# One state-space layer, re-planned: B and C sent out in a later step, the residual read late, seven decays ahead, moments in SBUF, one pair moved from GpSimd to VectorE

## The chip, the cores and the metric

The kernel runs on one core of a Trainium2 chip. A core has five engines that each take their instructions in order: TensorE (PE in the profile, with PEld for its weight loads), VectorE (DVE), ScalarE (ACT), GpSimd (POOL) and SyncE (SP), which here issues nearly all DMAs. They meet through semaphores: an instruction that waits holds up everything behind it on its engine. The metric is the device time of one execution in microseconds; less is better.

## What is computed

The input is x, of 4 images with 192 channels of 128 x 128 pixels. Layer 0 normalises x by groups and runs 1x1 convolutions, fractional Fourier transforms and inverse transforms on it. The second layer is a selective state-space block; the change touches only this one. The text calls it layer 2; in the code it is `layer1`. Cut to what matters:

```python
seq = layernorm(groupnorm(x))                    # tokens x 192
xs, z = split(seq @ in_proj_w.T)                 # 384 channels each
u  = silu(causal_conv4(xs) + conv_b)
dt, B, C = split(u @ x_proj_w.T)                 # rank 12, 16 states, 16 states
dt = softplus(dt @ dt_proj_w.T + dt_proj_b)
h[t] = h[t-1] * exp(dt[t] * A) + dt[t] * u[t] * B[t]     # 384 channels x 16 states
y[t] = sum over states of h[t] * C[t]  +  u[t] * D
out  = x + (y * silu(z)) @ out_proj_w.T
```

The recurrence in h runs over the 16,384 tokens of each image.

## The kernel before

Layer 2 goes through 128 chunks of 512 tokens (32 an image). The 384 channels are 3 blocks j of 128 partitions, the 16 states are 8 pairs sg. A chunk therefore has 24 steps k = 8 j + sg, and one step does a pair of states: two scans of 128 x 512 on VectorE (`scans`, L953), then one product of both with C on GpSimd (L966, `hc`), then sums over the states on TensorE three steps later (`sums`, L979, accumulated in PSUM by transposing). I number the states of a chunk 2 k and 2 k + 1.

A scan needs a decay exp(dt A) and an input dt u B. The decay is one Exp on ScalarE (L875). Where the input comes from is told by a letter in `KINDS`, one string of eight for each j:

- V: VectorE multiplies, one product of 128 x 512 for each state (`product`, L896), from a copy of dt u in PSUM (`dtu_copy`), two scans ahead.
- P: ScalarE scales a transposed dt u by B (`scale`, L924, tiles `dbT`, four for each state), and TensorE turns it back into PSUM (`turned_back`, L939), just ahead of its scan.
- O: GpSimd multiplies both states at once (`inputs`, L907, tile `db`), two steps ahead. Here the decay is written into PSUM (`decay_there`, tile `op`), three states ahead of its scan. For V and P it goes to SBUF (`early`, tile `da`), `AHEAD` = 4 decays ahead, into a ring of four.

The results of the scans, `h`, are in a ring of three, so step k waits until GpSimd and the carry's DMA have read h of step k - 3. The carry (L964) takes the last column of both scans out to the next chunk; it is a DMA of 1 KB on SP. B and C, of 64 KB, go out to DRAM (`xd_out`, L801) and come back spread over all partitions, 512 KB for each pair (`load_bc`, L844 and L848), behind the scans of steps 19 to 23 and 0 to 2.

Everything else is laid between these steps by a plan written out by hand. An entry of `PLAN` is a step, a phase, a function and its arguments. A step relative to a chunk's first one can be negative or over 23: the work of three chunks is interleaved. Inside a step the order is S (first), A (after the sums of an earlier step), then the first scan, M (between the two scans), the second scan, L (last). The work that the plan places for a chunk is, in its order: the load of x (`load_x`), the turn to tokens on TensorE, mean and variance (`moments`, L702 and L704), the reciprocal root by Ln and Exp (`rstd`), the normalising (`normed`, L725), the turn back to channels (`to_channels`), `channels` (L751; its second part also sends a shifted copy of `s` over SP, L757), the convolution (`conv`, L766), `silu_u` (L778), the gate's projection and activation (`proj_z` L772 and L773, `silu_z` L785), `proj_x` and `xd_out`, `proj_dt`, `softplus`, dt u on GpSimd (`dt_u`), the turns of B and of dt u, and at the end `evacuate` (`yt`, L988), `turn`, `gate` (L1011), `project_out` (L1018) and the residual's add (`add_x`, L1025) with the output's DMA (L1029).

ScalarE has Silu, Softplus and Exp with Ln in three different tables, so a change between them costs a table load. Five PSUM banks are handed from use to use in the order of the program, three more form the ring `op` for inputs and for the decays of kind O.

Of the kernel before, what the change touches and what calls it, by code (L numbers as in the profile page):

```python
# [10 lines left out]
F32 = mybir.dt.float32  # L11
I32 = mybir.dt.int32
BF16 = mybir.dt.bfloat16
AF = mybir.ActivationFunctionType
# [4 lines left out]
S = 128  # L19
C = 192  # L20
# [101 lines left out]
def layer0(tc, x, xmid, st2, w):  # L122
# [409 lines left out]

KINDS = ("VOPPVVOP", "VOVPOVPP", "VOVPPVOP")

PLAN = (
    (-35, "M", "load_x"), (-34, "M", "to_tokens", 1), (-34, "L", "to_tokens", 0),
    (-33, "L", "moments", 0), (-32, "A", "moments", 1), (-31, "L", "rstd"), (-30, "M", "shift"),
    (-30, "M", "normed", 0), (-30, "M", "normed", 1), (-30, "M", "to_channels", 1),  # L540
    (-29, "L", "to_channels", 0), (-29, "L", "channels", 0), (-27, "L", "channels", 1),
    (-26, "S", "conv", 0, 0), (-26, "L", "conv", 1, 0), (-25, "L", "conv", 1, 1),
    (-24, "L", "conv", 1, 2), (-22, "S", "conv", 0, 1), (-20, "S", "silu_u", 1),
    (-20, "S", "conv", 0, 2), (-20, "S", "silu_u", 0), (-20, "M", "conv", 2, 0),
    (-19, "M", "conv", 2, 1), (-17, "A", "conv", 2, 2), (-16, "L", "silu_u", 2),
    (-15, "L", "proj_z", 0), (-15, "L", "silu_z", 0), (-13, "S", "proj_x"), (-13, "M", "xd_out"),
    (-11, "M", "proj_dt"), (-10, "S", "softplus"), (-9, "M", "dt_u", 1), (-8, "S", "turn_b"),
    (-8, "M", "dt_u", 0), (-8, "M", "b_out"), (-4, "A", "turned", 0), (-2, "M", "scale", 0, 6),
    (-2, "L", "dtu_copy", 0), (-1, "A", "scale", 0, 4), (0, "A", "scale", 0, 5),
    (0, "M", "scale", 0, 15), (1, "S", "scale", 0, 7), (2, "M", "scale", 0, 14),  # L550
    (4, "S", "turned", 1), (7, "A", "dt_u", 2), (7, "A", "dtu_copy", 1), (7, "A", "scale", 1, 6),
    (7, "M", "scale", 1, 7), (9, "M", "scale", 1, 15), (10, "S", "proj_z", 1),
    (10, "A", "scale", 1, 14), (10, "L", "scale", 1, 13), (10, "L", "scale", 1, 12),
    (10, "L", "evacuate", 0), (11, "S", "proj_z", 2), (11, "M", "silu_z", 1),
    (11, "M", "silu_z", 2), (11, "L", "turn", 0), (13, "S", "gate", 0), (13, "A", "dtu_copy", 2),
    (17, "S", "turned", 2), (17, "S", "scale", 2, 6), (17, "M", "scale", 2, 7),
    (18, "M", "scale", 2, 8), (18, "M", "scale", 2, 9), (18, "M", "evacuate", 1),
    (19, "L", "scale", 2, 15), (20, "S", "scale", 2, 14), (21, "A", "turn", 1),
    (22, "S", "gate", 1), (27, "A", "evacuate", 2), (29, "S", "turn", 2), (29, "M", "gate", 2),
    (32, "S", "project_out", 0), (32, "L", "add_x", 0), (34, "S", "project_out", 1),  # L560
    (34, "L", "add_x", 1),
)

# [1 line left out]
def layer1(tc, xmid, out, st2, w, n_tok=S * S):  # L565
# [3 lines left out]
    NCHUNK = n_tok // T  # L569
    G = 2  # L570
    LAG, BCL = 3, 5
    AHEAD = 4
    NBLK = T // 128

    with ExitStack() as ctx:
# [26 lines left out]
        def done(g, *key):  # L602
            banks.append(g.pop(key)[1])
# [19 lines left out]
        for b in range(B):  # L623
            nc.sync.dma_start(
                out=gd[CH : CH + 1, b, :, :], in_=dnmr[:, b, :].rearrange("c t -> t c").unsqueeze(0)
            )
        xms = [cp.tile([CH + 1, 2, T], F32, name=f"xm{i}") for i in range(3)]
        for xm in xms:
            nc.vector.memset(xm[CH : CH + 1], 1.0)

        ln = const("ln")
        wz = cp.tile([128, 2, NJ, 128], F32, name="wz")
# [33 lines left out]
        def log_exp():  # L666
            if table[0] != "log_exp":
                nc.scalar.preload_act_table_set("natural_log_exp_and_others")  # L668
                table[0] = "log_exp"

        def load_x(i):
            b, ch = divmod(i, NCHUNK)
            xm = got[i]["xm"] = xms[i % 3]
            nc.sync.dma_start(
                out=xm[0:CH],
                in_=xmid[b][:, ch * T : (ch + 1) * T].rearrange("(t p) f -> p t f", p=CH),
            )

        def to_tokens(i, half):
            g = got[i]
            psum(g, "X", half)
            for blk in (2 * half, 2 * half + 1):
                for t in range(2):
                    nc.tensor.matmul(
                        row(g, blk)[:, t * CH : (t + 1) * CH],
                        g["xm"][:, t, blk * 128 : (blk + 1) * 128], gd[:, i // NCHUNK, t, :],
                        start=True, stop=True,
                    )  # L690

        def row(g, blk):
            return g["X", blk // 2][0][:, blk % 2 * C : (blk % 2 + 1) * C]

        def mean_var(g):
            return g["X", 1][0][:, 2 * C : 2 * C + 2 * NBLK].rearrange("p (k m) -> p k m", m=2)

        def moments(i, half):
            g = got[i]
            st = tp.tile([128, 2, 6], F32, name="st")  # L700
            for blk in range(2):
                nc.vector.bn_stats(st[:, blk, :], row(g, 2 * half + blk))  # L702
            for blk in range(2):
                nc.vector.bn_aggr(mean_var(g)[:, 2 * half + blk, :], st[:, blk, :])  # L704

        def rstd(i):
            g = got[i]
            rs = g["rs"] = tp.tile([128, NBLK], F32, name="rs")
            log_exp()
            nc.scalar.activation(rs, mean_var(g)[:, :, 1], AF.Ln, bias=eps)  # L710
            nc.scalar.activation(rs, rs, AF.Exp, scale=-0.5)

        def shift(i):
            g = got[i]
            sh = g["sh"] = tp.tile([128, NBLK], F32, name="sh")
            nc.vector.scalar_tensor_tensor(
                sh, mean_var(g)[:, :, 0], -1.0, g["rs"], ALU.mult, ALU.mult
            )

        def normed(i, half):  # L720
# [74 lines left out]
        def xd_out(i):  # L795
            g = got[i]
            xd = g["xd"] = tp.tile([128, T], F32, name="xd", bufs=1)
            nc.scalar.copy(xd, g["px",][0])
            done(g, "px")
            dbc = g["dbc"] = dram.tile([2, NS, T], F32, name="dbc")  # L800
            nc.sync.dma_start(out=dbc.rearrange("a s t -> (a s) t"), in_=xd[96:, :])  # L801

        def proj_dt(i):
            g = got[i]
# [3 lines left out]
                rows = slice(32 * j, 32 * j + RANK)  # L808
                nc.tensor.matmul(g["d", j][0], dtT[rows, :], g["xd"][rows, :], start=True, stop=True)

        def softplus(i):
            g = got[i]
            for j in range(NJ):
                g["dt", j] = jp.tile([128, T], F32, name="dt")
                nc.scalar.activation(g["dt", j], g["d", j][0], AF.Softplus, bias=dtb[:, j : j + 1])  # L815
                done(g, "d", j)
            table[0] = "softplus"

        def dt_u(i, j):
            g = got[i]  # L820
# [57 lines left out]
        def early(i):  # L878

            if i < len(own):  # L880
                decay(own[i], scp.tile([128, T], F32, name="da"))

        def decay_there(s):

# [56 lines left out]
        def scans(pos, n, k, between):  # L941
            g = got[n]
            j, sg = divmod(k, NG)
            ch = n % NCHUNK
            if k == 0:
                g["carry"] = tp.tile([128, NJ, NS], F32, name="carry")
                g["before"], last["carry"] = last.get("carry"), g["carry"]
            db = g.pop(("db", k), None)
            h = scp.tile([128, G, T], F32, name="h", bufs=3)
            for q in range(G):  # L950
                st = sg * G + q
                s = G * pos + q
                nc.vector.tensor_tensor_scan(  # L953
                    h[:, q, :], das.pop(s), dbs.pop(s) if db is None else db[:, q, :],
                    0.0 if ch == 0 else g["before"][:, j, st : st + 1], ALU.mult, ALU.add,
                )
                product(s + 2)
                decay_there(s + 3)
                if q == 0:
                    turned_back(s + 3)  # L960
                    between()
                if s in turns:
                    early(turns[s] + AHEAD)
            nc.sync.dma_start(out=g["carry"][:, j, sg * G : (sg + 1) * G], in_=h[:, :, T - 1])  # L964
            hc = scp.tile([128, G, T], F32, name="hc", bufs=5)
            nc.gpsimd.tensor_tensor(hc, h, g["c", "b", sg], ALU.mult)  # L966
            g["hc", k] = hc
# [53 lines left out]
                )  # L1021

        def add_x(n, t):
            xm = got[n]["xm"][0:CH]
            nc.vector.tensor_add(xm[:, t, :], got[n]["po", t][0][0:CH], xm[:, t, :])  # L1025
            done(got[n], "po", t)
            if t == 1:
                b, ch = divmod(n, NCHUNK)
                nc.sync.dma_start(  # L1029
                    out=out[b][:, ch * T : (ch + 1) * T].rearrange("(t p) f -> p t f", p=CH), in_=xm  # L1030
                )
                got[n] = None

        order = [(n, k) for n in range(total) for k in range(NGR)]
        does = dict(
            load_x=load_x, to_tokens=to_tokens, moments=moments, rstd=rstd, shift=shift,
            normed=normed, to_channels=to_channels, channels=channels, conv=conv, proj_z=proj_z,
            silu_u=silu_u, silu_z=silu_z, proj_x=proj_x, xd_out=xd_out, proj_dt=proj_dt, softplus=softplus, dt_u=dt_u,
            turn_b=turn_b, b_out=b_out, dtu_copy=dtu_copy, turned=turned, scale=scale,
            evacuate=evacuate, turn=turn, gate=gate, project_out=project_out, add_x=add_x,  # L1040
        )
# [193 lines left out]
```

## Time and profile before

| | |
|---|---|
| median of 3 runs | 11,175.64 us (11,174.62 to 11,181.45) |
| the profiled execution | 11,188.61 us, its span 11,186.7 us |
| first scan of layer 2 | 1,446 us after the span's start |
| scans L953, with a carry | 4,464 and 1,488, mean 1,268 and 1,267 ns |
| products with C, L966 | 3,072, mean 2,367 ns |
| products of kind O, L907 | 768, mean 2,373 ns |
| products of kind V, L896 | 2,304, mean 676 ns |
| scalings of kind P, L924 | 9,216, mean 396 ns |
| B, C loads to landing | 4.9 and 5.8 us |

A mean duration isn't the time that an instruction adds to a full engine: the next one begins before the last one ends. In the timeline, two scans follow each other at 1.18 us, a product behind a scan adds 0.59, a decay adds 0.615, and one dbT tile 0.25. Sums of work are made from such spacings. In the lines of waits the columns are the total in us, the number of waits and the longest one. In a timeline, the columns are the start, the length, the engine, the line, the operation and, in square brackets, the idle time before and who ended it.

### The profile page before, as it was taken

To read this page: it belongs to the slowest core of one execution; us is meant where nothing else is said; L and a number is where in the kernel's file an instruction comes from. 1 tells how busy PE (TensorE), PEld (TensorE's weight loads), DVE (VectorE), ACT (ScalarE), POOL (GpSimd) and SP (SyncE) were. 2 spreads that over 40 slices of the span, in tenths; PEclk is the share of its full clock that TensorE was granted. 3 is DMA by queue.
4 is the path that set the end of the run, shared out by engine and by line. 5 is a ranking of instruction groups with operands and counts; after the bars stand their busy time and mean duration, and the time that the engine had idled before them with its cause. 6 is when DMAs were issued, how large, how long until landed. Compare 5 with 4: busy or idle time off the path is not lost. (4 is left out here: it accounts for less than half of the span.)

```text
span 11186.7 us, 171424 instructions
## 1 busy us (share of the span) xinstructions
PE 9950.4 (89%) x56050; PEld 6911.8 (62%) x56050; DVE 10160.0 (91%) x11330; ACT 9542.3 (85%) x20197; POOL 9513.5 (85%) x4342
## 2 busy tenths in 40 slices
PE   4777789999999999999999999999999999999998
PEld 2434356666666666666666666666666666666666
DVE  5666679999999999999999999999999999999999
ACT  2333189999999999999999999999999999999998
POOL 0000079999999999999999999999999999999999
PEclk8888699999999999999999999999999999999999
DMA  8786733333333333333333333333343333333333
GB/s 234 187 225 163 220 98 114 117 105 109 117 105 110 117 105 109 117 112 102 118 117 97 119 119 95 118 119 99 114 119 101 113 117 106 109 117 107 107 117 92
DMA packets 1330364, 1366.48 MB, mean 122 GB/s; under 512 B 918346, under 2 KB 969791, under 8 KB 1328831
## 3 DMA queue, kind: packets, MB, share of 16 engines
q1 hardware_dynamic: 1308990, 1292.60, 39.8%
q0 software_dynamic: 13312, 50.34, 1.4%
q10 hardware_dynamic: 7168, 12.59, 0.3%
q8 instruction: 445, 7.29, 0.3%
q14 instruction: 449, 3.67, 0.1%
HBM read 1179.79 MB, written 155.33 MB: 119 GB/s over the span
## 5 line engine op out<-in xcount | busy, mean ns | idle before, releaser
L966 POOL TENSOR_TENSOR hc<-h,c 128x1024 f32<-128x1024 f32 x3072 | 7200.0, 2367 | 321.2 <-DVE h L953 240.8
L953 DVE TENSOR_TENSOR_SCAN h<-da,carry,op 128x512 f32<-128x512 f32 x4464 | 5532.7, 1268 | 281.0 <-ACT op L875 122.6
L875 ACT ACTIVATE da<-dt,c_A_log 128x512 f32<-128x512 f32 x4608 | 3218.5, 741 | 224.7 <-DVE h L953 216.0
L979 PE MATMUL ps<-ident,hc 128*128 128x128 f32 x24576 | 3258.2, 278 | 3.7 <-POOL hc L966 3.7
L979 PEld LDWEIGHTS ps<-ident,hc 128*128 128x128 f32 x24576 | 2874.5, 144 | 277.2 <-issue 272.2
L924 ACT ACTIVATE dbT<-ps,bT 128x128 f32<-128x128 f32 x9216 | 2583.6, 396 | 12.6 <-PE op L939 11.7
L766 PE MATMUL ps<-s,wc 128*128 128x512 f32 x4608 | 2184.4, 596 | 44.0 <-ACT u L778 36.4
L953 DVE TENSOR_TENSOR_SCAN h<-op,carry,db 128x512 f32<-128x512 f32 x1488 | 1853.4, 1267 | 98.0 <-DMA carry<-h 81.7
L907 POOL TENSOR_TENSOR db<-dtu,b 128x1024 f32<-128x1024 f32 x768 | 1822.5, 2373 | 7.4 <-DMA b<-dbc 7.4
L939 PE MATMUL op<-ident,dbT 128*128 128x128 f32 x9216 | 1422.6, 281 | 242.8 <-ACT dbT L924 168.8
L939 PEld LDWEIGHTS op<-ident,dbT 128*128 128x128 f32 x9216 | 1107.4, 144 | 752.1 <-issue 334.6
L896 DVE TENSOR_TENSOR op<-ps,b 128x512 f32<-128x512 f32 x2304 | 1556.5, 676 | 7.2 <-ACT ps L856 7.2
L875 ACT ACTIVATE op<-dt,c_A_log 128x512 f32<-128x512 f32 x1536 | 1092.0, 711 | 267.4 <-DVE h L953 267.2
L766 PEld LDWEIGHTS ps<-s,wc 128*128 128x128 f32 x4608 | 786.1, 190 | 634.2 <-issue 565.9
L1018 PE MATMUL ps<-yg,c_woT 128*96 128x512 f32 x1536 | 710.2, 599 | 7.6 <-ACT u L778 2.1
L668 ACT ACT_TABLE_LOAD x511 | 655.6, 1283 | 10.0 <-PEq L1225 0.7
L916 PE MATMUL ps<-ident,dtu 128*128 128x128 f32 x1536 | 262.4, 297 | 337.0 <-ACT bT L834 337.0
L822 POOL TENSOR_TENSOR dtu<-dt,u 128x512 f32<-128x512 f32 x384 | 490.6, 1278 | 57.9 <-ACT dt L815 57.9
L495 POOL DMA_DIRECT2D xmid<-xt x64 | 41.6, 651 | 573.2 <-DVE xt L491 528.8
L1018 PEld LDWEIGHTS ps<-yg,c_woT 128*96 128x96 f32 x1536 | 240.2, 163 | 447.7 <-issue 336.7
L916 PEld LDWEIGHTS ps<-ident,dtu 128*128 128x128 f32 x1536 | 179.2, 148 | 393.2 <-ACT bT L834 366.8
L202 DVE BATCH_NORM_STATS2 st<-xt 96x6 f32<-96x512 f32 x512 | 322.2, 677 | 101.7 <-DMA xt<-in_x 100.5
(166 smaller groups left out, 9818.2 us busy)
## 6 DMA issues: line engine op xcount, KB each, us to landing
c<-dbc SPq DMA_DIRECT2D x1024, 512.0 KB, 5.8
b<-dbc SPq DMA_DIRECT2D x768, 512.0 KB, 4.9
xt<-in_x SPq DMA_DIRECT2D x176, 768.0 KB, 8.4
xmid<-xt POOLq DMA_DIRECT2D x64, 768.0 KB, 5.5
xm<-xmid SPq DMA_DIRECT2D x128, 384.0 KB, 3.8
carry<-h SPq DMA_DIRECT2D x3072, 1.0 KB, 1.9
out<-xm SPq DMA_DIRECT2D x128, 384.0 KB, 3.2
s<-s SPq DMA_DIRECT2D x128, 128.5 KB, 2.3
```

Of the source, the lines that this page charges most:

```text
L668: nc.scalar.preload_act_table_set("natural_log_exp_and_others")
L766: nc.tensor.matmul(g["c", j][0], wc[:, j, k, :], rhs, start=k == 0, stop=k == 5)
L822: nc.gpsimd.tensor_tensor(g["dtu", j], g["dt", j], g["u", j], ALU.mult)
L875: nc.scalar.activation(da, got[n]["dt", j], AF.Exp, scale=A[:, j, st : st + 1])
L896: nc.vector.tensor_tensor(dbs[s], g["dp", j][0], g["b", k % NG][:, q, :], ALU.mult)
L907: nc.gpsimd.tensor_tensor(db, _bc(g["dtu", j], 1, G), g["b", sg], ALU.mult)
L924: nc.scalar.activation(t[:, blk, :], g["tu", j][0][:, at], AF.Identity, scale=g["bT"][:, blk, st : st + 1],)
L939: nc.tensor.transpose(db[:, blk * 128 : (blk + 1) * 128], t[:, blk, :], ident)
L953: nc.vector.tensor_tensor_scan(h[:, q, :], das.pop(s), dbs.pop(s) if db is None else db[:, q, :], 0.0 if ch == 0 else g["before"][:, j, st ...
L966: nc.gpsimd.tensor_tensor(hc, h, g["c", "b", sg], ALU.mult)
L979: nc.tensor.matmul(py[:, blk, :], hc[:, q, blk * 128 : (blk + 1) * 128], ident, start=first, stop=sg == NG - 1 and q == G - 1 and blk == N ...
L1018: nc.tensor.matmul(g["po", t][0][0:CH], woT[:, j, t * CH : (t + 1) * CH], g["yg", j], start=j == 0, stop=j == NJ - 1,)
```

## The change

- `KINDS`: in block j = 1, step 12 (sg = 4) goes from O to V. In block j = 2, steps 20 and 21 exchange V and P.
- `AHEAD` goes from 4 to 7, with a ring `da` of seven; the ring of `h` stays three.
- `xd_out` keeps the copy of x_proj's result; the DMA of B and C becomes a step of its own, `dbc_out`, placed two steps later (-12 and -10).
- x is loaded into one buffer `xm`, not three. The residual is read again from DRAM by `load_xr` into `xr` at step 28 of its chunk, four steps ahead of its first add.
- Mean and variance go to an SBUF tile `mv`, not into the tail of a PSUM bank. `rstd` writes its Ln to a tile of its own and its Exp twice: to SBUF for `normed`, and to PSUM for `shift`.
- `softplus` is one plan entry for each j.
- The plan places most of its entries anew. Those that the text speaks of are in the diff.

```diff
-KINDS = ("VOPPVVOP", "VOVPOVPP", "VOVPPVOP")
+BUFS = 7, 3
+KINDS = ("VOPPVVOP", "VOVPVVPP", "VOVPVPOP")
 PLAN = (
...
-    (-33, "L", "moments", 0), (-32, "A", "moments", 1), (-31, "L", "rstd"), (-30, "M", "shift"),
+    (-32, "S", "moments", 0), (-32, "L", "moments", 1), (-32, "L", "rstd"), (-30, "A", "shift"),
...
-    (-15, "L", "proj_z", 0), (-15, "L", "silu_z", 0), (-13, "S", "proj_x"), (-13, "M", "xd_out"),
-    (-11, "M", "proj_dt"), (-10, "S", "softplus"), (-9, "M", "dt_u", 1), (-8, "S", "turn_b"),
-    (-8, "M", "dt_u", 0), (-8, "M", "b_out"), (-4, "A", "turned", 0), (-2, "M", "scale", 0, 6),
+    (-15, "A", "proj_z", 0), (-15, "M", "silu_z", 0), (-13, "M", "proj_x"), (-12, "S", "xd_out"),
+    (-11, "M", "proj_dt"), (-10, "S", "dbc_out"), (-10, "A", "softplus", 0),
+    (-10, "M", "softplus", 1), (-10, "M", "softplus", 2), (-10, "L", "turn_b"),
+    (-10, "L", "b_out"), (-9, "L", "dt_u", 1), (-8, "L", "dt_u", 0), (-3, "L", "turned", 0),
...
-    (7, "M", "scale", 1, 7), (9, "M", "scale", 1, 15), (10, "S", "proj_z", 1),
-    (10, "A", "scale", 1, 14), (10, "L", "scale", 1, 13), (10, "L", "scale", 1, 12),
-    (10, "L", "evacuate", 0), (11, "S", "proj_z", 2), (11, "M", "silu_z", 1),
-    (11, "M", "silu_z", 2), (11, "L", "turn", 0), (13, "S", "gate", 0), (13, "A", "dtu_copy", 2),
+    (9, "M", "scale", 1, 14), (10, "M", "scale", 1, 13), (10, "L", "scale", 1, 15),
+    (10, "L", "evacuate", 0), (10, "L", "proj_z", 1), (11, "M", "proj_z", 2),
+    (11, "M", "silu_z", 1), (11, "M", "silu_z", 2), (11, "L", "scale", 1, 12),
+    (11, "L", "turn", 0), (12, "L", "gate", 0), (13, "M", "dtu_copy", 2), (16, "M", "turned", 2),
...
+    (26, "M", "evacuate", 2), (28, "M", "load_xr"), (28, "L", "turn", 2), (30, "L", "gate", 2),
+    (31, "S", "project_out", 0), (32, "L", "add_x", 0), (34, "S", "project_out", 1),
...
-        xms = [cp.tile([CH + 1, 2, T], F32, name=f"xm{i}") for i in range(3)]
+        xm = cp.tile([CH + 1, 2, T], F32, name="xm")
...
         def load_x(i):
+            nc.sync.dma_start(out=xm[0:CH], in_=chunk_of(xmid, i))
+
+        def load_xr(i):
+            xr = got[i]["xr"] = op.tile([CH, 2, T], F32, name="xr")
+            nc.sync.dma_start(out=xr, in_=chunk_of(xmid, i))
...
-                nc.vector.bn_aggr(mean_var(g)[:, 2 * half + blk, :], st[:, blk, :])
+                nc.vector.bn_aggr(g["mv"][:, 2 * half + blk, :], st[:, blk, :])
...
-            nc.scalar.activation(rs, mean_var(g)[:, :, 1], AF.Ln, bias=eps)
-            nc.scalar.activation(rs, rs, AF.Exp, scale=-0.5)
+            nc.scalar.activation(lnv, g["mv"][:, :, 1], AF.Ln, bias=eps)
+            g["rp"] = g["X", 1][0][:, 2 * C : 2 * C + NBLK]
+            nc.scalar.activation(rs, lnv, AF.Exp, scale=-0.5)
+            nc.scalar.activation(g["rp"], lnv, AF.Exp, scale=-0.5)
...
             done(g, "px")
+
+        def dbc_out(i):
+            g = got[i]
             dbc = g["dbc"] = dram.tile([2, NS, T], F32, name="dbc")
-            nc.sync.dma_start(out=dbc.rearrange("a s t -> (a s) t"), in_=xd[96:, :])
+            nc.sync.dma_start(out=dbc.rearrange("a s t -> (a s) t"), in_=g["xd"][96:, :])
...
-                decay(own[i], scp.tile([128, T], F32, name="da"))
+                decay(own[i], scp.tile([128, T], F32, name="da", bufs=AHEAD))
...
-            h = scp.tile([128, G, T], F32, name="h", bufs=3)
+            h = scp.tile([128, G, T], F32, name="h", bufs=H)
...
-            nc.vector.tensor_add(xm[:, t, :], got[n]["po", t][0][0:CH], xm[:, t, :])
+            xr = got[n]["xr"]
+            nc.vector.tensor_add(xr[:, t, :], got[n]["po", t][0][0:CH], xr[:, t, :])
```

## The prediction

> **What bounds the kernel now.** I read the page first, then the busy time by stretch of layer 2, VectorE's waits, and last the timeline of one chunk, because the first two name no single bound. A chunk is 24 steps of two scans.
>
> ```profile
> PE 9950.4 (89%) x56050; PEld 6911.8 (62%) x56050; DVE 10160.0 (91%) x11330; ACT 9542.3 (85%) x20197; POOL 9513.5 (85%) x4342
> ```
> ```profile
> 5000.00:6000.00 1000.00, 922.19 (x5419) 656.84 (x5418) 958.91 (x1061) 945.50 (x2036) 969.65 (x437) 0.98 0.36 110
> ```
> In a stretch of layer 2 four engines are 92 to 97% busy (after the length: PE, PEld, DVE, ACT, POOL). GpSimd is the fullest, but that isn't yet a bound: the question is who ends VectorE's waits.
>
> ```profile
> DVE h L953 <- ACT op L875: 25.9, 26, 1.2
> DVE h L953 <- DMA carry<-h: 18.4, 27, 1.3
> DVE h L953 <- PE op L939: 18.2, 33, 0.8
> DVE h L953 <- POOL hc L966: 8.5, 18, 1.4
> ```
> Over 5000 to 7000 us (26.4 chunks) GpSimd ends only 8.5 us of VectorE's waits. The three others end 62. The page's chain covers about 1% of the span, so I traced the loop by hand through the chunk that starts at 6014.3:
>
> ```profile
> 6043.32 0.69 ACT L778 ACTIVATE u<-ps,c_cb 128x512 f32<-128x512 f32 x1
> ...
> 6068.28 0.69 ACT L875 ACTIVATE op<-dt,c_A_log 128x512 f32<-128x512 f32 x1 [0.42 <-DVE h L953]
> ...
> 6086.29 0.81 ACT L751 ACTIVATE s<-ps,c_ln 64x512 f32<-64x512 f32 x1
> ```
> ```profile
> 6044.06 2.81 PE L1018 MATMUL ps<-yg,c_woT 128*96 128x512 f32 x6
> ...
> 6048.44 0.60 PE L939 MATMUL op<-ident,dbT 128*128 128x128 f32 x4
> ...
> 6060.59 0.66 PE L939 MATMUL op<-ident,dbT 128*128 128x128 f32 x4
> ```
> ```profile
> 6049.24 1.28 DVE L953 TENSOR_TENSOR_SCAN h<-da,carry,op 128x512 f32<-128x512 f32 x1 [0.99 <-ACT op L875]
> ...
> 6061.45 1.28 DVE L953 TENSOR_TENSOR_SCAN h<-da,carry,op 128x512 f32<-128x512 f32 x1 [0.47 <-PE op L939]
> ...
> 6094.64 2.46 DVE L953 TENSOR_TENSOR_SCAN h<-op,carry,db 128x512 f32<-128x512 f32 x2 [1.19 <-POOL hc L966]
> ```
> ```profile
> 6055.84 0.33 SPq L801 DMA_DIRECT2D dbc<-xd  x1
> ...
> 6087.13 0.51 SPq L757 DMA_DIRECT2D s<-s  x1
> 6087.69 1.23 SPq L844 DMA_DIRECT2D b<-dbc  x1
> 6089.00 0.38 SPq L848 DMA_DIRECT2D c<-dbc  x1
> 6089.48 0.60 SPq L964 DMA_DIRECT2D carry<-h  x1
> ```
> What to see, piece by piece (in brackets the mean over 95 chunks, cut at the same instructions):
> 1. From the end of step 8's scans (6041.2) to the decay at 6068.28 [27.1 us]. ScalarE loads a table, makes `u` and so frees a PSUM bank. PE then runs without a gap: output projection, gate projection, the turn for step 11 (6048.44, so the 0.99 is PE's, though the line names ScalarE), and on to the turn for step 15 (6060.59, wait 0.47). VectorE sets off from there, and ScalarE waits for it: 0.42 [0.46].
> 2. From there ScalarE is full up to `channels` part 1, ending 6087.1 [18.4]; one wait for PE ahead of the copy of `yt`, 0.48 [0.16].
> 3. SP sends `s`, one B and one C load, then step 22's carry. That carry is queued behind 1 MB, and step 1's scan needs the h buffer it reads: 6094.64 [7.1; the carry takes 5.1 to land].
> 4. Step 1 to step 8 on VectorE, nearly without waits [23.3].
> The sum is 75.9 us a chunk; 128 chunks make 9,720 of the 11,186.7.
>
> [...] 1024 columns take 2.37 us at L907, 2 x 0.68 at L896; start to start 2.32 against 1.17. [...]
>
> **The change, part by part** (us a chunk).
> - One pair of step 12 goes from kind O to V. GpSimd loses one L907, 2.32: its work falls from 73.5 to 71.2. VectorE gains two L896, 1.17: its work (75.95 less 3.27 idle) rises from 72.7 to 73.85. That is below the loop, so it costs only where VectorE sets the loop. In piece 1 it does so after the turn for step 15, and the products lie before that: they fill time that VectorE waited.
> - B and C sent out later. SP stands still for some 6.7 us before 6055.84, waiting for `xd`, with steps 11 and 12's carries behind it. Now step 13's carry and the x load go ahead. This takes away step 14's carry wait, 0.17; step 15's turn is late next, so 0 on the loop.
> - Gate projections 1 and 2 move behind the turns for step 11. The turn for step 11 comes 1.7 earlier and the 0.99 goes. But PE's work between `u` and the turn for step 15 is the same set of matmuls, so that turn still lands about 20.2 after step 8's end. VectorE alone would need 19.45 now, so about 0.75 of wait stays there.
> - Half of the moments (2 x 0.27 + 2 x 0.22 = 1.0) moves past step 16's first scan. VectorE then gets there 20.2 + 3.5 + 1.0 + 1.2 = 25.9 after step 8's end, before 27.1.
> - ScalarE's own queue now sets piece 1: 27.1 less its wait of 0.46, plus `bT` 0.1, which moves into the piece: 26.7. Same decays (27 up to `channels` 1), same 40 dbT tiles, same eight table loads a chunk: the split softplus adds none, for no decay of kind O falls between its parts.
> - Piece 2: 18.4, less the PE wait 0.16 (its column sums now have two more dbT groups ahead of the copy), less `bT` 0.1, plus the second Exp into PSUM 0.11 to 0.2: 18.3.
> - Piece 3: SP's order around the chunk's edge is the same: 7.1.
> - Piece 4: 23.3, less step 3's wait for a decay, 0.1, which seven decays ahead remove: 23.2. The decay still waits for the same scan, so ScalarE starts none earlier; only its due time moves.
> - Moments in SBUF: four L704 of 0.19; unknown side, at most +-0.1. Taken as 0.
> - The residual's load: 384 KB and one SP issue of 0.56 between the carries of steps 3 and 4; x's same load lands in 3.8, step 8's add is some 12 us later. Behind it, carry 4 may land some 2 later and has 4 of slack at step 7. Cost 0; 0.3 at most if C loads crowd it.
>
> Sum: 26.7 + 18.3 + 7.1 + 23.2 = 75.3 against 75.9, a gain of 0.6. I keep 0.5, since half of PE's wait and some of ScalarE's may come back in single chunks. 128 x 0.5 = 64. The profiled execution took 11,188.6, so it would take 11,124. The median of the runs is 13 lower, so 11,175.6 - 64, about **11,110**. The fill ahead of the first scan (three more decays of 0.62) stays within 2 us.
>
> **Rivals.**
> - *Given back.* The loop keeps its 75.9, because PE, not ScalarE, ends piece 1: for it, the matmul run after `u` is the same; against it, 0.8 lies between 25.9 and 26.7. Time 11,175, within 25.
> - *VectorE becomes the bound.* If ScalarE's lead gets `channels` 1 done early enough that the carry no longer waits behind the loads, then 73.85 + 0.75 = 74.6, a gain of 1.35 x 128 = 173: 11,003. Against it: in my count `channels` 1 ends at step 22's end, 0.4 later by VectorE's clock than now.
> - *Slower: a ring between PE and ScalarE in steps 11 to 14.* The dbT group for state 28 now stands behind two table loads, two gate activations and two decays (4.8 us more) and is done 15.5 after step 8's end; PE's turn reads it at 16.3. Now it is ready 5.8 ahead. The gate activations in turn wait for the gate projections that PE now runs later (done 9.1 and 10.85, read at 10.75 and 11.25). If ScalarE is L late there, the turns for 14 and 15 are L - 0.85 late, with a wait of 0.75 + L - 0.85. Where VectorE rules piece 1, the chunk is 74.1 plus that wait: no cost until it passes 1.3, slower than before from 1.9 (L = 2.0). At a wait of 2.6 the chunk is 76.7: +0.75 x 128 = 96, so 11,270.
> - *The change doesn't do what it says*, seven ahead giving no lead: that is already my reading.
>
> **How the numbers follow.** Forecast 0.55, VectorE bound 0.15, given back 0.13, slower 0.17. A measurement of this kernel tells about 0.2% (22 us) from no change. Faster 0.70, same 0.13, slower 0.17. The forecast's own range is 11,050 to 11,150; with half of the deep gain and of the slow case in it, 11,020 to 11,220.
>
> **What would show it.** Right: step 11's wait gone; a wait of 0.4 to 1 for PE at step 15; no ScalarE wait for VectorE at the decay for step 17; step 1 still held by the carry, by 1 us or more; `dbc` sent without SP standing; L907 640 times, L896 2560; GpSimd idle about 4 us a chunk. Wrong: new waits for L939 at steps 14 and 15 of 2 us together; or step 1's carry wait gone.

## The result, and the profile after

The changed kernel takes 11,251.98 us (median of 4 runs, 11,243.74 to 11,257.67), the kernel before 11,175.56 beside it (4 runs, 11,174.62 to 11,181.45): a ratio of 1.0065, 95% interval 1.0049 to 1.0081. The forecast was 11,110. The profiled execution took 11,243.74 us, its span 11,241.9. The mean chunk went from 75.98 to 76.57 us, and 128 x 0.59 = 76 is as much as the two medians differ by.

The page of the changed kernel, its first part and three groups of its fifth (each kernel's lines have its own numbers: the scans, L953 before, are L963 here):

```profile
PE 10027.9 (89%) x56050; PEld 7049.9 (63%) x56050; DVE 10262.2 (91%) x11584; ACT 9562.5 (85%) x20325; POOL 9222.5 (82%) x4214
...
L906 DVE TENSOR_TENSOR op<-ps,b 128x512 f32<-128x512 f32 x2560 | 1727.9, 675 | 11.3 <-ACT ps L866 5.9
...
L917 POOL TENSOR_TENSOR db<-dtu,b 128x1024 f32<-128x1024 f32 x640 | 1515.3, 2368 | 6.0 <-DMA b<-dbc 5.8
...
L998 ACT COPY yt<-ps 128x512 f32<-128x512 f32 x384 | 226.3, 589 | 275.4 <-PE ps L989 274.2
```

GpSimd lost 291 us of work, VectorE gained 102, the counts (2,560 and 640) are those of the diff. PE has the same 56,050 matmuls, yet was busy 78 us longer: they ran slower. New is the idle time of ScalarE ahead of the copy of `yt`, 275 us. In a stretch of layer 2 (PE, PEld, DVE, ACT, POOL, then the granted clock) no engine is fuller than before except PE with its weight loads, and the clock is 0.96 where it was 0.98:

```profile
5000.00:6000.00 1000.00, 929.34 (x5373) 671.34 (x5372) 957.53 (x1073) 936.96 (x2018) 928.52 (x418) 0.96 0.39 115
```

VectorE's waits over 5000 to 7000 us, the first four, and then ScalarE's wait for the column sums, before and after:

```profile
DVE yg L1021 <- PE ps L1014: 24.9, 26, 1.3
DVE h L963 <- DMA carry<-h: 19.3, 24, 2.2
DVE h L963 <- PE op L949: 16.0, 40, 0.5
DVE h L963 <- issue: 12.3, 15, 1.5
```
```profile
ACT yt L988 <- PE ps L979: 5.5, 11, 0.7
ACT yt L998 <- PE ps L989: 51.9, 48, 2.4
```

Step 11's wait for `op` (25.9 before) is gone. In its place VectorE waits once a chunk for gate 1 (`yg`, step 21), which reads what TensorE turns back from `yt`. ScalarE's wait for the column sums was 5.5 us in 11 cases before, 51.9 in 48 now. About half of it is the copy in step 2 of the next chunk (1.0 us a chunk now, 0.04 before), where VectorE sets the loop; that half stays in the faster versions below (0.8 to 1.3).

The prediction cut the loop into four pieces. Their means over the same steady chunks:

| piece | before | predicted | after |
|---|---|---|---|
| 1: end of step 8's scans to the decay for step 17 | 27.1 | 26.7 | 26.7 |
| 2: to the end of `channels` 1 | 18.4 | 18.3 | 19.5 |
| 3: to step 1's scan | 7.2 | 7.1 | 7.1 |
| 4: step 1 to step 8 | 23.3 | 23.2 | 23.3 |

Piece 2 is the miss: 1.2 us a chunk, of which 1.1 is the wait of the copy in step 18 (0.15 before). The timeline of PE and then of ScalarE there, in one chunk:

```profile
6154.48 0.60 PE L926 MATMUL ps<-ident,dtu 128*128 128x128 f32 x4
6154.92 1.04 PE L989 MATMUL ps<-ident,hc 128*128 128x128 f32 x8
6159.94 1.09 PE L949 MATMUL op<-ident,dbT 128*128 128x128 f32 x4 [3.98 <-DVE h L963]
6160.82 1.92 PE L989 MATMUL ps<-ident,hc 128*128 128x128 f32 x8
6162.52 0.93 PE L949 MATMUL op<-ident,dbT 128*128 128x128 f32 x4
...
6167.81 1.04 PE L989 MATMUL ps<-ident,hc 128*128 128x128 f32 x8
```
```profile
6162.77 0.58 ACT L998 COPY yt<-ps 128x512 f32<-128x512 f32 x1 [1.32 <-PE ps L989]
```

PE turns dtu 2, does the sums of one more step, and stands for 3.98 us, because its next instruction, a turn of `dbT`, needs a ring buffer that step 17's scans still read. After that the turn takes 1.09 us where four such matmuls take 0.60, and the eight sums 1.92 where they take 1.04. The copy of `yt` needs these sums. The stretches of 4 us around it (length, the five engines, then the granted clock, third from the end) say why:

```profile
6154.00:6158.00 4.00, 1.96 (x18) 1.72 (x16) 4.00 (x8) 4.00 (x9) 4.00 (x3) 1.00 0.04 0
6158.00:6162.00 4.00, 2.06 (x10) 2.09 (x11) 4.00 (x7) 3.41 (x15) 4.00 (x3) 0.72 0.04 0
6162.00:6166.00 4.00, 3.33 (x20) 2.49 (x19) 4.00 (x5) 3.23 (x7) 3.54 (x3) 0.85 0.04 0
```

Before, PE idled about as long at this place, but in two parts with work between them, and the copy didn't wait:

```profile
6146.18 0.66 PE L916 MATMUL ps<-ident,dtu 128*128 128x128 f32 x4 [2.59 <-ACT bT L834]
...
6149.53 0.63 PE L939 MATMUL op<-ident,dbT 128*128 128x128 f32 x4 [1.81 <-ACT dbT L924]
```
```profile
6151.71 0.63 ACT L988 COPY yt<-ps 128x512 f32<-128x512 f32 x1
```

The first part was the wait of `turned` 2 behind `turn_b` for the copy of B. The change moves B two steps earlier and `turned` 2 half a step, so this work is done ahead of the idle and the two parts become one. In the changed kernel's chunk shown above, the trace has the clock granted at 0.5 from 6159.79 on, 3.83 us after the sums end at 6155.96, for 3.41 us. Such stretches, of 3.4, 6.8 or 10.2 us, are in 119 of 121 chunks after; before, of 3.4 or 6.8 us, in 78 of 121. The gaps that they follow are counted in the last section.

### The profile page after: what moved, and what is told of

Same layout as the page of the kernel before. It is cut to its first block, busy times and chain, and to the rows that moved or that the text cites. A ratio compares the mean times of both kernels' runs of the same rounds, so it can differ in the third digit from the quotient of the medians.

```text
span 11241.9 us, 171927 instructions
## 1 busy us (share of the span) xinstructions
PE 10027.9 (89%) x56050; PEld 7049.9 (63%) x56050; DVE 10262.2 (91%) x11584; ACT 9562.5 (85%) x20325; POOL 9222.5 (82%) x4214
## 5 line engine op out<-in xcount | busy, mean ns | idle before, releaser
L963 DVE TENSOR_TENSOR_SCAN h<-da,carry,op 128x512 f32<-128x512 f32 x4712 | 5845.4, 1267 | 155.9 <-PE op L949 77.8
L885 ACT ACTIVATE da<-dt,c_A_log 128x512 f32<-128x512 f32 x4864 | 3396.1, 738 | 76.8 <-DVE h L963 69.6
L949 PE MATMUL op<-ident,dbT 128*128 128x128 f32 x9216 | 1500.1, 288 | 603.6 <-DVE h L963 583.1
L906 DVE TENSOR_TENSOR op<-ps,b 128x512 f32<-128x512 f32 x2560 | 1727.9, 675 | 11.3 <-ACT ps L866 5.9
L963 DVE TENSOR_TENSOR_SCAN h<-op,carry,db 128x512 f32<-128x512 f32 x1240 | 1542.3, 1269 | 106.3 <-DMA carry<-h 47.6
L917 POOL TENSOR_TENSOR db<-dtu,b 128x1024 f32<-128x1024 f32 x640 | 1515.3, 2368 | 6.0 <-DMA b<-dbc 5.8
L885 ACT ACTIVATE op<-dt,c_A_log 128x512 f32<-128x512 f32 x1280 | 907.5, 709 | 223.2 <-DVE h L963 222.5
L998 ACT COPY yt<-ps 128x512 f32<-128x512 f32 x384 | 226.3, 589 | 275.4 <-PE ps L989 274.2
L1004 PE MATMUL ps<-ddp,u 128*128 128x128 f32 x3072 | 446.6, 293 | 0.0
L1004 PEld LDWEIGHTS ps<-ddp,u 128*128 128x128 f32 x3072 | 415.6, 210 | 0.0
```

Source lines behind the costliest of these rows:

```text
L885: nc.scalar.activation(da, got[n]["dt", j], AF.Exp, scale=A[:, j, st : st + 1])
L906: nc.vector.tensor_tensor(dbs[s], g["dp", j][0], g["b", k % NG][:, q, :], ALU.mult)
L917: nc.gpsimd.tensor_tensor(db, _bc(g["dtu", j], 1, G), g["b", sg], ALU.mult)
L949: nc.tensor.transpose(db[:, blk * 128 : (blk + 1) * 128], t[:, blk, :], ident)
L963: nc.vector.tensor_tensor_scan(h[:, q, :], das.pop(s), dbs.pop(s) if db is None else db[:, q, :], 0.0 if ch == 0 else g["before"][:, j, st ...
L1004: nc.tensor.matmul(got[n]["py", j][0][:, blk * 128 : (blk + 1) * 128], got[n]["u", j][:, blk * 128 : (blk + 1) * 128], ddp[:, j, :], start ...
```

## The experiments

Theory A: the joined idle lowers PE's clock, the sums after it are late, and the copy of `yt` in step 18 holds ScalarE. Theory B: it is the pair given to VectorE. Theory C: ScalarE comes to the copy too soon, with one group of `dbT` fewer ahead of it, and would wait there at any clock. Ratios are to the kernel before on the same chip; the last columns are means over 121 chunks of each trace, in us: the time for which the clock was granted at one half, the wait of the copy of `yt` in step 18, and the length of the chunk.

| run | ratio, interval | low clock a chunk | wait of `yt` | chunk |
|---|---|---|---|---|
| before | | 3.3 | 0.15 | 75.98 |
| after | 1.0065 (1.0049 to 1.0081) | 5.8 | 1.08 | 76.57 |
| e1_warm | 0.9965 (0.9952 to 0.9977) | 1.6 | 0.23 | 75.65 |
| e2_swap18 | 0.9936 (0.9923 to 0.9950) | 5.9 | 0.00 | 75.30 |
| e8_bT_late | 0.9955 (0.9943 to 0.9968) | 1.2 | 0.19 | 75.50 |
| e4_kinds | 1.0100 (1.0086 to 1.0113) | 6.2 | 1.29 | 76.80 |
| e9_before_bT | 1.0079 (1.0067 to 1.0092) | 6.4 | 0.56 | 76.61 |
| e13_before_bT_warm | 1.0019 (1.0012 to 1.0026) | 3.1 | 0.23 | 76.11 |
| e3_loads | 1.0096 (1.0083 to 1.0110) | 6.5 | 1.59 | 76.79 |
| e5_ahead4 | 1.0094 (1.0079 to 1.0110) | 6.1 | 1.24 | 76.71 |
| e10_swap_late | 0.9926 (0.9914 to 0.9939) | 3.4 | 0.00 | 75.23 |
| e11_swap_late_loads | 1.0002 (0.9994 to 1.0010) | 3.2 | 0.00 | 75.95 |
| e14_dbc_at_once | 0.9916 (0.9903 to 0.9929) | 3.3 | 0.00 | 75.29 |
| e15_best_ahead4 | 0.9922 (0.9909 to 0.9934) | 3.4 | 0.00 | 75.21 |

**e1_warm**: the changed kernel with PE's idle partly filled.

```diff
-                nc.tensor.transpose(g["tu", j][0][:, at], g["dtu", j][:, at], ident)
+                for _ in range(5 if j == 2 else 1):
+                    nc.tensor.transpose(g["tu", j][0][:, at], g["dtu", j][:, at], ident)
```

> The changed kernel with one addition: the turn of dt u for block 2, in step 16, does its four transposes five times over into the same PSUM bank (1.7 us more of PE work a chunk, same values), which fills most of the 3.98 us in which PE stands before the turn for step 19. Theory A (PE's clock): the loss is the half clock that the record grants after that one long idle stretch, so that the column sums ahead of ScalarE's copy yt take twice as long. Then the low-clock time falls from 6.0 us a chunk to under 1.5, the copy's wait from 1.1 to under 0.4, the chunk from 76.5 to about 75.6: 11,130 (-120). Theory B (VectorE's two more products are the loss): no change, 11,250. Theory C (one dbT group fewer ahead of the copy, so that ScalarE waits there at any clock): no change in the wait, 11,250.

Sixteen useless matmuls more in each chunk, and the median is 11,117.5, below the kernel before (11,157.2). PE's waits in this trace:

```profile
PE op L950 <- DVE h L964: 80.4, 80, 2.2
```

No wait of PE is over 2.2 us any more. In the 80 chunks without a low stretch the chunk is 75.21; in 25 with one of 3.4 us it is 76.07, in 16 with one twice as long 77.19. The copy waits 0.23 where it waited 1.08, with the same groups of `dbT` ahead of it: theory A holds, and B and C, which expected no change, fall as explanations by themselves. The wait also follows the clock chunk by chunk. Where the clock was at one half for over 0.8 of the 4 us ahead of the copy, it waits 0.97 us on average (26 chunks), elsewhere 0.03 (95); in the changed kernel these means are 1.20 (108 chunks) and 0.12 (13).

**e2_swap18**: the clock left as it is, the copy freed.

```diff
+                if k == 18 and pos >= LAG:
+                    sums(*order[pos - LAG])
                 turned_back(G * (pos + 1))
-                if pos >= LAG and sg != LAG:
+                if pos >= LAG and sg != LAG and k != 18:
                     sums(*order[pos - LAG])
```

> The changed kernel with two pieces of PE's queue exchanged in step 18 of each chunk: the sums of step 15 before the turn for step 19, which waits for the end of step 17's scans. Theory A and C both: the sums are done about 3 us earlier, the copy's wait (1.1) goes, ScalarE is ahead by that: the chunk falls from 76.5 to 75.4 to 75.6, 11,110 to 11,130. Under A the low clock falls too, since the idle stretch is cut in two; under C it need not. Theory B: no change, 11,250.

The sums that `yt` needs no longer stand behind the turn that waits for VectorE. PE and ScalarE at this place:

```profile
6155.14 0.63 PE L949 MATMUL op<-ident,dbT 128*128 128x128 f32 x4 [2.76 <-DVE h L963]
6156.98 1.09 PE L949 MATMUL op<-ident,dbT 128*128 128x128 f32 x4 [1.21 <-DVE h L963]
```
```profile
6156.48 0.67 ACT L998 COPY yt<-ps 128x512 f32<-128x512 f32 x1
```

The clock still falls (1.09 for a turn, 5.9 us a chunk at half clock, as much as in the changed kernel), yet the copy waits for nothing and the chunk takes 75.30. So here the low clock's cost is in what waits for PE, and that is the copy of `yt` (1.08 us a chunk in the changed kernel, 0.00 here). I had expected the low clock to go too under theory A, and it didn't; taken alone, e2 fits theory C as well. That the sums are late because of the clock rests on e1, e8 and e9.

**e8_bT_late**: the changed kernel with B and `turned` 2 where they were before.

```diff
-    (-10, "L", "turn_b"), (-10, "L", "b_out"),
+    (-8, "S", "turn_b"), (-8, "M", "b_out"),
...
-    (16, "M", "turned", 2),
+    (17, "S", "turned", 2),
```

> The changed kernel with three plan entries put back where they were before: the turn of B at -8 S, its copy bT at -8 M, the turn of dt u for block 2 at 17 S. PE then waits for bT first and for step 17's end later, two shorter stretches, as before the change. Theory A: low clock 3 to 4 us a chunk (3.5 before the change, 6.0 after), the copy's wait down by half, 11,190 to 11,210. Theories B and C: no change, 11,240 to 11,260.

```profile
6171.20 0.66 PE L926 MATMUL ps<-ident,dtu 128*128 128x128 f32 x4 [2.15 <-ACT bT L844]
...
6174.46 0.63 PE L949 MATMUL op<-ident,dbT 128*128 128x128 f32 x4 [1.73 <-DVE h L963]
```

The idle is in two parts again, the low stretches are gone from 93 of 121 chunks, and the kernel takes 11,110.6 against 11,157.2. It came out better than I had written. Everything in the change but this move gains 0.45%; the move costs the 1.1% between 0.9955 and 1.0065.

**e4_kinds**: the pair of step 12 given back to GpSimd.

```diff
-KINDS = ("VOPPVVOP", "VOVPVVPP", "VOVPVPOP")
+KINDS = ("VOPPVVOP", "VOVPOVPP", "VOVPVPOP")
```

> The changed kernel with step 12 back at kind O: GpSimd makes its inputs again (768 products L907, 2304 on VectorE). Theory B: VectorE loses 1.17 us of work a chunk and the time falls by up to 150, to 11,100. Theory A: those products lie ahead of step 15, where PE's run of matmuls sets the time, and the idle stretch of PE is untouched: within 25 of 11,252.

Slower than the changed kernel, by about 0.35%, each taken beside the kernel before on its own chip. Theory B falls: the pair on VectorE costs nothing. VectorE's first wait there doubles against the changed kernel (24.9 us in 26 cases): each chunk has a second gate that comes too early for PE.

```profile
DVE yg L1021 <- PE ps L1014: 48.8, 52, 1.3
```

Of the 0.23 us by which the chunk is longer, however, 0.21 is the copy of `yt`, which waits 1.29 for 1.08. So the 0.35% is what the pair brings beside a late copy; what it brings where the copy isn't late was not tried.

**e9_before_bT**: the reverse of e8, the kernel before with only this move made.

```diff
-(-9, "M", "dt_u", 1), (-8, "S", "turn_b"), (-8, "M", "dt_u", 0), (-8, "M", "b_out"),
+(-9, "M", "dt_u", 1), (-10, "L", "turn_b"), (-10, "L", "b_out"), (-8, "M", "dt_u", 0),
...
-    (17, "S", "turned", 2),
+    (16, "M", "turned", 2),
```

> The kernel before, with only the turn and copy of B moved two steps earlier and the turn of dtu 2 half a step earlier, as in the changed kernel. Theory A (PE's two short waits ahead of steps 17 to 19 join into one[...], the clock drops each time, and the late column sums hold the copy yt): granted clock down from .954 to about .945, the copy yt waits 0.4 to 0.6 us a chunk where it waited 0.16, and the time rises by 20 to 60 us, so 11,175 to 11,220 where the kernel before takes 11,157. Rival (where B is turned is harmless by itself; it needs the change's later VectorE): within 20 of 11,157. Rival (B earlier is good by itself): below 11,135.

```profile
6155.19 1.09 PE L939 MATMUL op<-ident,dbT 128*128 128x128 f32 x4 [4.93 <-ACT rs L710]
```
```profile
6158.02 0.59 ACT L988 COPY yt<-ps 128x512 f32<-128x512 f32 x1 [0.60 <-PE ps L979]
```

One idle of 4.93 us, a turn at half clock behind it, and `yt` waits: the mechanism appears in the old kernel too. (The line names ScalarE's `rs`, which this turn doesn't read; in each of the 121 chunks the turn begins 0.15 us after the end of step 17's scans, as it does in the changed kernel.) I had its size too small, 20 to 60 us for 88. The copy's 0.4 is the larger part of the 0.63 us a chunk; another 0.2 is at step 3, whose scan now waits for a turn by PE.

**e13_before_bT_warm**: e9 with the five transposes of e1.

> The kernel before with B turned early (which alone took it to 1.0079 of before), and the sixteen... of PE's idle filled: the transposes of dtu 2 made five times. Theory A (it is the clock after the joined idle): granted clock back to .96 or more and the time within 25 us of the kernel before. Rival (B's place in the queues of PE and ScalarE costs, whatever the clock): still 1.005 or more of before.

The clock is back at .957, as in the kernel before, and the ratio falls from 1.0079 to 1.0019: three quarters of what the move costs there is the idle. The interval of the last 0.2% excludes zero. In the trace it lies in piece 4 (23.4 for 23.3), where step 3's scan waits 0.16 for a turn by PE that it didn't wait for before; which of the moved entries makes that turn late wasn't tried.

**e3_loads**: the loads of B and C ahead of a step's late work. They then don't stand behind `s`, which waits for ScalarE; they leave sooner, and so does step 22's carry, which is still behind them.

```diff
+                if k >= NGR - BCL and n + 1 < total:
+                    load_bc(n + 1, k - (NGR - BCL))
+                if k < NG - BCL and n:
+                    load_bc(n, k + BCL)
                 act(pos, "L")
```

> The changed kernel, with one step's B and C loads sent ahead of that step's late work instead of behind it, so that the scale rows s and step 22's carry stand in another order on SP. If step 1's carry wait (0.4 us a chunk, 0.2 more at step 3) is on the path: the changed kernel would take about 11,230 on this chip and this one 11,160 to 11,200. Theory A says that wait is late only because piece 2 is late by 1.1 us, and that ScalarE's channels 1 would hold the next chunk anyway: 11,210 to 11,240, with the copy yt still waiting 1.1 us.

Slower than the changed kernel, by 0.3%, and above both ranges. Step 1's scan does come 0.8 us sooner after `channels` 1 (6.28 for 7.09), but piece 1 as VectorE runs it grows from 25.7 to 26.2 and `yt` waits 1.59. With the low clock taken out of the way (**e11_swap_late_loads**) the loss remains:

> The best version so far (column sums ahead in step 18, B turned late: 0.9926 of before) with the B and C loads sent ahead of the step's late work. In the changed kernel this cut the way from channels 1 to step 1 from 7.05 to 6.28 us, and gave it back elsewhere. If what it gave back was the low clock at yt: now a gain of up to 0.7 us a chunk, 0.985 to 0.990 of before. If it was the scale rows s that wait behind the loads (PE waited 2.0 us for them): 0.991 to 0.996.

PE's waits and the DMAs of e11 (columns of the latter: KB each, median us to landing):

```profile
PE ps L774 <- DMA s<-s: 31.6, 21, 3.1
```
```profile
carry<-h SPq DMA_DIRECT2D x3072, 1.0 KB, 1.9
...
s<-s SPq DMA_DIRECT2D x128, 128.5 KB, 5.8
```

Now `s` stands behind the loads: it lands in 5.8 us where it took 2.4 without the reordering, and PE's convolution waits for it. The turn for step 2 is behind that convolution: in the median chunk step 2's scan begins 3.36 us after it, and this scan waits 0.93 us a chunk, where it waits 0.01 in e10. The chunk loses 0.7 us, more than either reading had allowed. Step 22's carry gains nothing in e11: the 1.9 us are the median over the carries of all steps, and this one takes 5.5 to land (5.1 in the changed kernel). Of `s` and the loads, `s` is the more urgent, and the old order is right.

**e10_swap_late**: e2 and e8 together.

> Both remedies at once: step 18's column sums ahead of the turn, and B turned late as before. If the copy yt's wait is the whole miss (either remedy alone takes it to 0.2 or less), the two don't add: 11,075 to 11,095, as with the sums alone (11,084), though the clock rises from .940 to about .968. If the low clock costs by itself, elsewhere too: 11,040 to 11,065.

11,070.3 against 11,152.0. The two don't add: 0.9926 stands beside 0.9936, and 2.5 more microseconds a chunk at full clock change the chunk by 0.07. The time lies between the two ranges, and the clock rose only to .954, so a small cost of the low clock by itself isn't excluded. VectorE's first waits:

```profile
DVE h L963 <- DMA carry<-h: 14.4, 23, 1.8
DVE h L963 <- PE op L949: 12.3, 27, 0.5
```

This version beats both kernels. Two parts of the change were undone on top of it. **e14_dbc_at_once** sends B and C out in the step of the copy again:

```diff
-    (-15, "A", "proj_z", 0), (-15, "M", "silu_z", 0), (-13, "M", "proj_x"), (-12, "S", "xd_out"),
-    (-11, "M", "proj_dt"), (-10, "S", "dbc_out"), (-10, "A", "softplus", 0),
+    (-15, "A", "proj_z", 0), (-15, "M", "silu_z", 0), (-13, "M", "proj_x"), (-12, "S", "xd_out"), (-12, "S", "dbc_out"),
+    (-11, "M", "proj_dt"), (-10, "A", "softplus", 0),
```

> The same best version with B and C sent out in the step of x_proj's copy again, as before the change. The prediction put the later send-out at 0 on the loop, with step 14's carry wait, 0.17 us, under cover of PE's wait at step 15: 0.9915 to 0.994 of before. If SP's standing does cost: up to 0.17 a chunk, 22 us, so 0.995.

0.9916: the later send-out is worth nothing on the loop, as predicted.

**e15_best_ahead4** and, on the changed kernel itself, **e5_ahead4** put the decays four ahead:

```diff
-BUFS = 7, 3
+BUFS = 4, 3
```

> The same best version with the decays four ahead. The prediction gave the seven 0.1 us a chunk (step 3's wait for a decay), 13 us: 0.993 to 0.995. If the seven bring ScalarE a lead: 0.996 or more. If nothing: 0.9915 to 0.993.

> The changed kernel with the decays four ahead again in place of seven. If the lead does nothing (the prediction: the decays wait for the same scans, 0.1 us a chunk at most at step 3): 11,220 to 11,250 where the changed kernel takes about 11,230. If the seven bring a lead of their own: above 11,270. If they cost, by putting ScalarE's decays ahead of what PE waits for: below 11,210.

On the best version nothing changes (0.9922). On the changed kernel the ratio is 1.0094 where the changed kernel has 1.0065; the two intervals touch, and the time is in none of the three ranges. The chunk is 0.14 longer, and the copy of `yt` waits 0.16 longer (1.24 for 1.08). e15, where that copy doesn't wait, gives no support to a gain from the seven. I count it as nothing, with that doubt left.

## Why the prediction was wrong

- **The step that failed** is in piece 2: "18.4, less the PE wait 0.16 (its column sums now have two more dbT groups ahead of the copy)". Instead of going, the wait grew to 1.1 us. Two errors are in it. The count was wrong: one dbT group fewer stands ahead of the copy and one more behind it (from the copy to the end of `channels` 1 it is 12.87 us now, 11.77 before), so ScalarE came to the copy sooner. And the sums came later: I counted the earlier `bT` as 0.1 us of ScalarE's work, and didn't ask what PE would do in the time in which it used to wait for it. e1 and e8, which shorten and split the joined idle, and e2, which frees the sums, each take the wait to 0.23 or less and the time below the kernel before. The runs weigh the two errors: with the low clock and the old count (e9) the copy waits 0.56, with the new count and little low clock (e1, e8) 0.23 and 0.19, with both 1.08. The copy put back behind one more group, at the low clock, wasn't tried.
- **Piece 1 right.** Predicted 26.7, measured 26.7. Step 11's wait went, step 15's turn still lands about 20.1 us after step 8's end (predicted 20.2), VectorE waits 0.46 for it (predicted 0.4 to 1), and ScalarE no longer waits for VectorE at the decay for step 17. Its table loads are still eight a chunk, of 1.28 us each in both traces. VectorE gets through step 16's first scan 25.7 after step 8's end, predicted 25.9.
- **Piece 3 and 4 right**: 7.1 and 23.3 for 7.1 and 23.2. The sign to look for was only half met: step 1's wait is 0.81, of it 0.39 for the carry and the rest for ScalarE, not 1 or more for the carry. In piece 4 the 0.1 that seven decays ahead were to take from step 3 isn't there: this step waited 0.12 before, 0.04 of it for a decay, and waits 0.17 now, for the carry. Of the other signs, L907 and L896 have their counts, and `dbc` no longer holds up SP (its waits for it in 2,000 us fell from 176.8 us to 4.2).
- **The pair** was placed as filling VectorE's idle time; e4 confirms that it costs nothing. **Later B and C** and **seven ahead**, put at 0 and 0.1: e14 and e15 show nothing.
- **The slower rival** gave 11,270 by waits at steps 14 and 15. The time is near by chance: no wait appears at step 14, and step 15's is 0.46.
- **The size of the rest.** With the failed step mended, the chunk falls by 0.5 (e8, 75.50) and by 0.75 (e10, 75.23), for a predicted 0.5: 0.9955 and 0.9926 of before, where 11,110 would have been 0.994.

The residual's late load, the moments in SBUF and the regrouped gate projections weren't undone one at a time; together with the pair they are in the 0.45% of e8.

## What to carry to other kernels

Idle time on an engine off the path is not free to be moved (e9: 1.0079): where work moves out of a gap of TensorE, look whether two short gaps become one. Here the clock was granted at one half within or behind a gap of 4.0 us in 119 of 121 chunks, and behind one of 2.2 us in 41; the first turn after the gap of 3.98 us took 1.09 us for 0.60. Ask then which instruction right behind the gap another engine waits for, and place it ahead of the wait; here that brought as much as keeping the clock up (0.9936 in e2, 0.9955 in e8). Before changing the order of transfers on one queue, find out which engine waits for each of them, not only for the one that is to gain.

## What the runs showed that was not expected

- The clock fell at gaps of 2.1 us as well, and in more chunks the longer the gap was. Counting the half-clock stretches that begin within or after PE's first gap over 0.5 us at this place, and before the next one: gaps of 2.1 us (e8) have one in 25 of 121 chunks, 2.2 (e1) in 41, 2.7 (the kernel before) in 70, 4.0 (the changed kernel) in 119, 4.7 (e9) in 121. So in the kernel before, the first gap alone was mostly enough, without the second. What decides in which chunks a gap of 2 to 3 us lowers the clock, these runs don't show. In 88 chunks of e10 the stretch comes only after three gaps, of 2.1, 0.9 and 1.2 us.
- Half a clock costs next to nothing here where no one waits: it is granted for 5.9 us of a 75 us chunk in e2 and for 3.4 in e10, the copy of `yt` waits for nothing in both, and their chunks differ by 0.07 us.
- Useless work can pay: in e1 sixteen transposes a chunk turn a loss of 0.65% into a gain of 0.35%.
